# Softplus of q spread over the loop over k, a sixth of its copies on ScalarE, and row sums copied first

## The chip, the cores and the metric

The kernel runs on one core of a Trainium2 chip. The metric is the device time of one execution in microseconds; the time of the kernel before is the median of three runs. The profile is of one such execution. Its engines are TensorE (PE, with its weight loads as PEld), VectorE (DVE), ScalarE (ACT), GpSimd (POOL) and SyncE (SP), which here issues most of the DMAs.

## The reference, cut to what matters

Eight images of 256 channels and 96 x 96 pixels go through two residual layers. Layer 0 is attention between channels in the frequency domain; layer 1 is linear attention over pixels. Both begin with a group norm.

```python
# layer 0: per head of 32 channels, q, k, v are 2D FFTs of 1x1 convolutions of gn(x)
attn = einsum('bhcn,bhdn->bhcd', l2norm(q_f), l2norm(k_f)) * temperature
attn = complex(softmax(real(attn)), softmax(imag(attn)))
out  = abs(ifft2(einsum('bhcd,bhdn->bhcn', attn, v_f)))
x    = x + pconv(out, w_out)
# layer 1: q and k have 32 channels, v has 256; xf is gn(x) as (B, C, N)
q = softplus(einsum('dc,bcn->bnd', Wq, xf) + bq)
k = softplus(einsum('dc,bcn->bdn', Wk, xf) + bk)
v = einsum('ec,bcn->ben', Wv, xf) + bv
attn_map = einsum('bdn,ben->bde', k, v)
norm = 1.0 / einsum('bnd,bd->bn', q, sum(k, -1) + EPS)
x = x + einsum('bnd,bde,bn->ben', q, attn_map, norm)
```

## The kernel before

The kernel never builds the FFTs. The logits of layer 0 come from the covariance of the even and odd parts of the image, which `pair_sums` gathers (e and o are the sum and the difference of an image and its point reflection). `rotate` turns each row pair of the image by a table `tm`, which gives an image y whose channel mixing yields the absolute value of the inverse FFT; with it comes one more column per row, the row sums `ys`. `images` mixes and projects them; `layer1` and `output` are the second layer.

Each stage is a generator, and `weave` runs steps of another stage between its parts: `yield n` lets n steps of the other stage in. So the sums of image b + 1 run between the parts of `layer1(b)` and `output(b)`, and the rotation of image b between the parts of `attention(b)`. The last image has no sums beside it. A scheduler orders the instructions of each engine from this, outside the stretches that set the order by hand.

At the start, VectorE makes the constant tables before the first sums:

```python
nc.vector.reduce_sum(rep4[:, 0:D], ident.rearrange("p (j d) -> p d j", d=D), axis=AX.X)
# ... (copies to rep4, sel8)
nc.vector.memset(xT, 1.0)
# ...
for j in range(4):                       # 12 copies, of a table that a DMA brings
    o = HEAD * j
    nc.vector.tensor_copy(gsel[:, 0:16, j], gri[:, o:o + 16])
    # ...
pcs = ps_tile("pcs")                     # two small matmuls, and the rotation table from them
for c in range(2):
    nc.tensor.matmul(pcs[0:H, c:c + 1], lhsT=csn[0:1, c, :], rhs=ones[0:1, 0:1], start=True, stop=True)
```

The sums: each block u of rows gets e and o (L308, and L309 for the first column), four transposes (L341), a copy by ScalarE (L344), and the products `acc` (L322) of the block before.

```python
eng = nc.vector if u in (0, 1, NT) or b == 0 and u % 2 else nc.gpsimd
op(d[:, :, lo:hi, 1:W], x_t[:, :, ra:ra + n, 1:W], x_t[:, :, back, W - 1:0:-1])      # L308
# ... in pair_sums, for each block and each 128 columns:
nc.tensor.transpose(pt[0:np_, ...], eo[:, c, k, i:i + np_], ident)                   # L341
nc.scalar.activation(t[0:np_, :, 0:C], pt[0:np_, :]..., AF.Copy, scale=weight)       # L344
if pending is not None:
    products(*pending, first, False)                                                 # L322
```

In `attention`, the softmax of the two halves m of the heads ends in the matmuls `at` (L485), with steps of the rotation let in ahead of each:

```python
            yield (5, 2)[m]
            pa = ps_tile(f"at_{b}_{m}")
            nc.tensor.matmul(pa[:, 0:4 * NZ], lhsT=sbd, rhs=gsel..., start=True, stop=True)
```

The end of a step of `rotate`, and the first matmuls of `images` that read `ys`:

```python
nc.vector.tensor_copy(y[:, :, :, g:g + 2], src[:, :, W - 1::-1, :])     # L550
nc.vector.tensor_copy(ys[:, :, g:g + 2], src[:, :, W, :])               # L551
# images: zs = mz^T ys (L583); then the z matmuls on y (L612)
```

Layer 1, with softplus and the loop over k (six turns s of three blocks i):

```python
yield 1.5

def softplus(c, s):                      # c = 0: k, c = 1: q; z holds max(a, 0), e holds exp(-|a|)
    nc.vector.tensor_scalar_add(u, e, 1.0)                                              # L735
    nc.vector.scalar_tensor_tensor(e, in0=u, scalar=1.0, in1=e, op0=ALU.subtract, op1=ALU.subtract)  # L736
    nc.scalar.activation(u, u, AF.Ln, bias=zero)                                        # L737
    nc.vector.tensor_sub(z, z, e)                                                       # L738
    nc.vector.tensor_add(z, z, u)                                                       # L739
# ...
softplus(0, 0)
for s in range(NS):
    if s + 1 < NS:
        softplus(0, s + 1)
    if s >= NS // 2:
        for i in (0, 1):
            softplus(1, 2 * s - NS + i)
    # transpose k of turn s (kT, L764), copied by ScalarE (L765)
    for i in range(s * CH // P, (s + 1) * CH // P):
        for jj in range(2):
            # eight transposes of x (xT, L773)
            if jj:
                nc.scalar.copy(xt[jj][:, :, 0:C], src)                                  # L776
            else:
                nc.vector.tensor_copy(xt[jj][:, :, 0:C], src)                           # L778
        if len(pend) == 2:
            for p in pend:
                add_kx(*p)               # kx += k^T x (L746)
            pend = []
        pend.append((i, xt, ...))
        yield 0.25
```

All transposes and most products pass through one pool of five PSUM tiles (`ps_tile`), so a transpose also waits until the tile of five allocations before is copied out.

Of the kernel before, what the change touches and what calls it, by code (L numbers as in the profile page):

```python
# [54 lines left out]
P = 128  # L55
KC = 2
HEAD = 32
D = 32
# [10 lines left out]
def two_layer_kernel(ctx: ExitStack, tc: tile.TileContext, x, w1t, b1, w2t, b2, w3, b3, wot, temp,  # L69
# [56 lines left out]
    def ps_tile(name):  # L126
        return psum.tile([P, 512], F32, tag="ps", name=name)
# [28 lines left out]
        nc.vector.memset(mask4[s, 12 + j:D + 4:4], 1.0)  # L156
        nc.vector.memset(esel[s, j:j + 1], 1.0 / HEAD)
    rep4 = const.tile([P, P], F32, name="rep4")
    nc.vector.reduce_sum(rep4[:, 0:D], ident.rearrange("p (j d) -> p d j", d=D), axis=AX.X)
    for j in range(1, 4):  # L160
        nc.vector.tensor_copy(rep4[:, 32 * j:32 * j + 32], rep4[:, 0:D])
    sel8 = const.tile([P, 8 * D], F32, name="sel8")
    nc.vector.tensor_copy(sel8.rearrange("p (i d) -> p i d", d=D), rep4[:, 0:8].unsqueeze(2).to_broadcast([P, 8, D]))
    NX = 6
    xT = const.tile([P, NX, 2, C + 2], F32, name="xT")
    nc.vector.memset(xT, 1.0)
    turn = [0, 0]

    def xt_slot(sums=False):
# [8 lines left out]
    nc.scalar.dma_start(out=gavg_sb, in_=gavg)  # L178
    gri = setup[:, 6 * W:6 * W + 2 * P]
    nc.scalar.dma_start(out=gri, in_=gmat)  # L180
    for j in range(4):
        o = HEAD * j
        nc.vector.tensor_copy(gsel[:, 0:16, j], gri[:, o:o + 16])
        nc.vector.tensor_copy(gsel[:, 17:32, j], gri[:, P + o + 1:P + o + 16])
        nc.vector.tensor_copy(gsel[:, 32, j:j + 1], gri[:, o + 16:o + 17])
    half = const.tile([P, 1], F32, name="half")
    nc.vector.memset(half, 1.0)
    nc.vector.memset(half[0:W], 0.5 ** 0.5)
# [42 lines left out]


    rt = dram.tile([H, 2 * W], F32, name="rt")
    pcs = ps_tile("pcs")
    for c in range(2):
        nc.tensor.matmul(pcs[0:H, c:c + 1], lhsT=csn[0:1, c, :], rhs=ones[0:1, 0:1], start=True, stop=True)
    cs = t0[:, 5 * W:5 * W + 2]
    nc.vector.tensor_copy(cs, pcs[0:H, 0:2])
    r0 = t0[:, 2 * W:3 * W]
    nc.vector.tensor_scalar_mul(t0[:, 0:W], t0[:, 0:W], cs[:, 0:1])  # L240
    nc.vector.scalar_tensor_tensor(r0, in0=t0[:, W:2 * W], scalar=cs[:, 1:2], in1=t0[:, 0:W], op0=ALU.mult, op1=ALU.add)
    for i in range(2):
        o = (3 + i) * W
        nc.vector.tensor_copy(t0[:, o:o + 1], r0[:, 0:1])
        nc.vector.tensor_copy(t0[:, o + 1:o + W], r0[:, W - 1:0:-1])
    nc.sync.dma_start(out=rt, in_=t0[:, 3 * W:5 * W])
    load_small()

    def window(h):

# [37 lines left out]
    def even_odd(b, u):  # L288

        nr = PR if u < NT else 1  # L290
        t = ring_tile(f"eo_{b}_{u}").rearrange("p (c k n) -> p c k n", c=2, k=KC)
        x_t = image(x_of(b))
        rows = [PR * u + i for i in range(nr)]
        if u in (0, NT):
            parts = [(0, 1)] + ([(1, nr)] if nr > 1 else [])
        else:
            parts = [(0, nr)]
        for lo, hi in parts:
            n = hi - lo
            ra = x_col(rows[lo]) // W  # L300
            rp = x_col((H - rows[lo]) % H) // W
            back = slice(rp, rp - n if rp >= n else None, -1)
            for c in range(2):
                eng = nc.vector if u in (0, 1, NT) or b == 0 and u % 2 else nc.gpsimd
                op = (eng.tensor_add, eng.tensor_sub)[c]
                pop = (nc.gpsimd.tensor_add, nc.gpsimd.tensor_sub)[c]
                d = t[:, c, :, 0:nr * W].rearrange("p k (h w) -> p k h w", w=W)
                op(d[:, :, lo:hi, 1:W], x_t[:, :, ra:ra + n, 1:W], x_t[:, :, back, W - 1:0:-1])  # L308
                pop(d[:, :, lo:hi, 0:1], x_t[:, :, ra:ra + n, 0:1], x_t[:, :, back, 0:1])  # L309
        return t, nr * W  # L310
# [50 lines left out]
    def attention(b):  # L361
# [105 lines left out]
        for m in range(KC):  # L467
            l = two.tile([P, HEAD], F32, tag="l", name=f"l_{b}_{m}")
            for j in range(4):
                s = slice(32 * j, 32 * j + 32)  # L470
                nc.vector.tensor_mul(l[s, :], lg[m][s, s], rk[s, m * P + 32 * j:m * P + 32 * j + 32])
            nc.vector.tensor_scalar_mul(l, l, rq[:, m:m + 1])
            nmax = two.tile([P, 1], F32, tag="nmax", name=f"nmax_{b}_{m}")
            nc.vector.reduce_max(nmax, l, axis=AX.X, negate=True)
            ssum = two.tile([P, 1], F32, tag="ssum", name=f"ssum_{b}_{m}")
            nc.scalar.activation(l, l, AF.Exp, bias=nmax, accum_out=ssum)
            nc.vector.reciprocal(ssum, ssum)
            sbd = scr[0][:, 5 * C + m * P:5 * C + (m + 1) * P]
            nc.gpsimd.memset(sbd, 0.0)
            for j in range(4):  # L480
                s = slice(32 * j, 32 * j + 32)
                nc.vector.tensor_scalar_mul(sbd[s, s], l[s, :], ssum[s, :])
            yield (5, 2)[m]
            pa = ps_tile(f"at_{b}_{m}")
            nc.tensor.matmul(pa[:, 0:4 * NZ], lhsT=sbd, rhs=gsel.rearrange("p n h -> p (n h)"), start=True, stop=True)  # L485
            nc.vector.tensor_copy(at[:, m, 0:NZ, 4 * m:4 * m + 4], pa[:, 0:4 * NZ].rearrange("p (n h) -> p n h", h=4))
            nc.vector.tensor_add(at[:, m, 16, 4 * m:4 * m + 4], esel, pa[:, 64:68])
# [33 lines left out]
    def rotate(b):  # L521

        y = image(y_of(b))
        ys = one.tile([P, KC, H + 1], F32, tag="ys", name=f"ys_{b}")

        def load_r(h):
            tm = three.tile([P, TR * (W + 1)], F32, tag="tm", name=f"tm_{b}_{h}")[0:W].rearrange("p (r w) -> p r w", r=TR)
            (nc.scalar if b else nc.sync).dma_start(out=tm[:, :, 0:W], in_=window(h))
            nc.gpsimd.tensor_copy(tm[:, :, W:W + 1], csn[0:W, 2, h:h + TR].unsqueeze(2))  # L529
            return tm  # L530

        def step(h, turned):

            if h is not None:
                pt = ps_tile(f"xr_{b}_{h}")
            if turned is not None:
                g, gt, tm = turned
                pu = ps_tile(f"y_{b}_{g}")
            for r in range(2):
                for k in range(KC):  # L540
                    if h is not None:
                        o = x_col(h + r)
                        nc.tensor.transpose(pt[0:W, r * C + k * P:r * C + (k + 1) * P], x_of(b)[:, k, o:o + W], ident)  # L543
                    if turned is not None:
                        o = (r * KC + k) * (W + 1)
                        nc.tensor.matmul(pu[:, o:o + W + 1], lhsT=gt[0:W, r, k * P:(k + 1) * P], rhs=tm[:, g % TR + r, :],  # L546
                                         start=True, stop=True)
            if turned is not None:
                src = pu[:, 0:2 * KC * (W + 1)].rearrange("p (r k w) -> p k w r", r=2, k=KC)
                nc.vector.tensor_copy(y[:, :, :, g:g + 2], src[:, :, W - 1::-1, :])  # L550
                nc.vector.tensor_copy(ys[:, :, g:g + 2], src[:, :, W, :])  # L551
            if h is not None:
                xt = xt_slot()
                nc.scalar.copy(xt[0:W, :, 0:C], pt[0:W, :].rearrange("p (r n) -> p r n", r=2))  # L554
                return xt

        tms = [load_r(g) for g in range(0, 3 * TR, TR)]
        pending = []
        for h in range(0, H, 2):
            if h % TR == 0:  # L560
                tm = tms.pop(0)
            if h % TR == 4 and 3 * TR <= h - 4 + 2 * TR < H:
                tms.append(load_r(h - 4 + 2 * TR))
            xt = step(h, pending.pop(0) if len(pending) == 2 else None)
            pending.append((h, xt, tm))
            yield
        for p in pending:
            step(None, p)
        y0[b] = ys
# [101 lines left out]
    def layer1(b):  # L671
# [53 lines left out]
            nc.tensor.matmul(pv[:, 0:C], lhsT=nmb[:, k, :], rhs=wvs[:, k, :], start=(k == 0), stop=(k == KC - 1))  # L725
        nc.vector.tensor_add(bvs, bvs, pv[:, 0:C])

        yield 1.5

        def softplus(c, s):  # L730

# [24 lines left out]
        for s in range(NS):  # L756
            if s + 1 < NS:
                softplus(0, s + 1)
            if s >= NS // 2:
                for i in (0, 1):  # L760
                    softplus(1, 2 * s - NS + i)
            pk = ps_tile(f"kT_{b}_{s}")
            for i in range(CH // P):
                nc.tensor.transpose(pk[:, i * P:(i + 1) * P], kq(0, s)[:, i * P:(i + 1) * P], ident)  # L764
# [1 line left out]
            for i in range(s * CH // P, (s + 1) * CH // P):  # L766
                xt = [slots[2 * (i % 3) + jj] for jj in range(2)]
                for jj in range(2):
# [3 lines left out]
                        for k in range(KC):  # L772
                            nc.tensor.transpose(pt[:, j * C + k * P:j * C + (k + 1) * P], x[:, k, o:o + P], ident)  # L773
                    src = pt.rearrange("p (j n) -> p j n", j=2)
                    if jj:
                        nc.scalar.copy(xt[jj][:, :, 0:C], src)  # L776
                    else:
                        nc.vector.tensor_copy(xt[jj][:, :, 0:C], src)  # L778
                if len(pend) == 2:
                    for p in pend:  # L780
                        add_kx(*p)
                    pend = []
# [102 lines left out]
    def finish(stage):  # L885
        for _ in stage:
            pass

    finish(pair_sums(0))
    turns = rotate(0)  # L890
    for b in range(B):
        with tc.manual_schedule(engines={mybir.EngineType.PE}):
# [60 lines left out]
```

## Time and profile before

| | |
|---|---|
| time, median of 3 (lowest, highest) | 2787.41 us (2787.17, 2787.41) |
| span of the profiled execution | 2783.2 us |
| mean granted TensorE clock | 0.998 |
| period of one image | 342.5 us |
| HBM read and written | 113.85 MB, 75.57 MB |

The zs matmuls of two images that follow each other start 342.5 us apart (497.0 us, 839.75 us and so on), which gives the period. By line, the largest shares of the chain that ended last are the z and the projection matmuls of `images` (20% and 18%), the products of the sums (13%) and the rotation (10% and 6%); the transposes of x in the loop over k have 4%, its products kx 2%.

A line of a timeline begins with the start and the length in us; then come engine, source line, operation, tiles written and read, shape and count. Brackets hold the idle time of that engine ahead of it and what ended that. Lines of source in the profile are those of the kernel before; in the changed kernel the same statements stand a few lines lower or higher.

### The profile page before, as it was taken

What the parts mean: (1) busy time and instruction counts of PE and PEld (TensorE: products, weight loads), DVE (VectorE), ACT (ScalarE), POOL (GpSimd) and SP (SyncE); (2) the same over time, 40 slices, a digit from 0 to 9 for tenths busy, and PEclk for the clock granted to TensorE, in tenths of its full rate; (3) what the DMA queues carried; (4) which work ended last, traced back from release to release, by engine and by line L of the source; (5) the groups of instructions that cost most, each with busy time, mean ns of one, the idle gap of its engine ahead of it and who ended that gap; (6) DMA issues with size and microseconds to landing.
All of it is one profiled execution on the core that took longest, in us unless ns stands there. A gap on an engine that the chain in (4) does not pass through costs nothing.

```text
span 2783.2 us, 47916 instructions
## 1 busy us (share of the span) xinstructions
PE 2725.0 (98%) x18460; PEld 1969.4 (71%) x18460; DVE 1986.8 (71%) x4122; ACT 1350.2 (49%) x2066; POOL 858.6 (31%) x928
## 2 busy tenths in 40 slices
PE   8999999999999999999999999999999999999987
PEld 7965679656795667956679566785668856788545
DVE  6578775877658776587675876758766687666767
ACT  3455534555345553455533555345454455544553
POOL 4033430343303434034240351403514135131321
PEclk9999999999999999999999999999999999999999
DMA  5120061201512015120151201512015210151003
GB/s 167 36 67 12 25 204 40 69 10 43 183 43 72 5 48 177 44 70 7 47 180 43 69 6 53 177 48 60 7 53 181 53 51 7 55 181 30 1 6 137
DMA packets 197810, 192.52 MB, mean 69 GB/s; under 512 B 89360, under 2 KB 197584, under 8 KB 197584
## 3 DMA queue, kind: packets, MB, share of 16 engines
q1 hardware_dynamic: 130336, 164.34, 18.6%
q10 hardware_dynamic: 67248, 25.12, 3.5%
q8 instruction: 147, 2.41, 0.4%
q14 instruction: 79, 0.65, 0.1%
HBM read 113.85 MB, written 75.57 MB: 68 GB/s over the span
## 4 chain that ended last, share of the span: by engine, by line
PE 92%; DVE 4%; ACT 2%; issue 1%; POOL 0%; DMA 0%; POOLq 0%; DVEq 0%; ACTq 0%
PE z L612 20%; PE po L624 18%; PE acc L322 13%; PE y L546 10%; PE xr L543 6%; PE eoT L341 5%; PE kq L709 5%; PE xT L773 4%; PE o L855 3%; PE kx L746 2%; DVE arena L739 1%; PE cw L420 1%; DVE arena L550 1%; PE kT L764 1%; PE mz L507 1%
## 5 line engine op out<-in xcount | busy, mean ns | idle before, releaser
L612 PE MATMUL z<-arena,mz 128*128 128x384 f32 (+2 forms) x2400 | 595.0, 476 | 0.0
L624 PE MATMUL po<-e,wo 128*128 128x384 f32 x1536 | 529.7, 486 | 0.2 <-ACT e L659 0.2
L658 POOL TENSOR_TENSOR e<-e 128x768 f32<-128x768 f32 x192 | 348.5, 1817 | 553.7 <-ACT e L657 553.7
L612 PEld LDWEIGHTS z<-arena,mz 128*128 128x128 f32 (+1 forms) x2400 | 325.7, 163 | 241.4 <-issue 42.4
L546 PE MATMUL y<-tm,xT 96*128 96x97 f32 x3072 | 477.0, 261 | 1.8 <-ACT sd_a L280 0.5
L546 PEld LDWEIGHTS y<-tm,xT 96*128 96x128 f32 x3072 | 462.6, 192 | 12.4 <-ACT xT L554 5.2
L322 PE MATMUL acc<-xT 128*128 128x256 f32 (+2 forms) x2368 | 440.6, 328 | 0.0
L624 PEld LDWEIGHTS po<-e,wo 128*128 128x128 f32 x1536 | 289.5, 190 | 197.7 <-DVE arena L626 1.2
L653 DVE TENSOR_TENSOR e<-z,xT 128x768 f32<-128x768 f32 x384 | 366.1, 953 | 88.4 <-PE z L612 88.4
L256 DVE BATCH_NORM_STATS2 st<-arena 128x6 f32<-128x384 f32 x768 | 406.1, 552 | 12.6 <-DMA arena<-in_x_dram 2.2
L543 PE MATMUL xr<-ident,arena 128*96 128x128 f32 x1536 | 413.6, 275 | 0.0
L322 PEld LDWEIGHTS acc<-xT 128*128 128x128 f32 (+1 forms) x2368 | 380.1, 191 | 35.7 <-issue 2.9
L550 DVE COPY arena<-y 128x384 f32<-128x384 f32 x384 | 213.9, 557 | 209.2 <-PE y L546 203.1
L554 ACT COPY xT<-xr 96x512 f32<-96x512 f32 x384 | 222.2, 583 | 283.3 <-PE xr L543 278.9
L308 POOL TENSOR_TENSOR eo<-arena 128x760 f32<-128x760 f32 x150 | 273.4, 1823 | 258.2 <-issue 133.6
L657 ACT ACTIVATE e<-e 128x1536 f32<-128x1536 f32 x192 | 284.5, 1482 | 93.2 <-DVE e L653 92.1
L659 ACT ACTIVATE e<-e 128x768 f32<-128x768 f32 x192 | 162.0, 844 | 334.2 <-POOL e L658 333.2
L626 DVE TENSOR_TENSOR arena<-arena,po 128x384 f32<-128x384 f32 x384 | 211.3, 552 | 94.7 <-PE po L624 71.8
L344 ACT ACTIVATE xT<-eoT 128x512 f32<-128x512 f32 x280 | 167.5, 598 | 180.6 <-PE eoT L341 178.9
L529 POOL COPY tm<-csn 96x6 f32<-96x6 f32 x128 | 24.2, 192 | 726.7 <-PE y L546 548.7
L543 PEld LDWEIGHTS xr<-ident,arena 128*96 128x96 f32 x1536 | 230.1, 150 | 8.9 <-issue 5.6
L341 PE MATMUL eoT<-ident,eo 128*128 128x128 f32 (+1 forms) x1184 | 186.8, 280 | 8.2 <-DVE eo L308 5.3
(201 smaller groups left out, 2932.2 us busy)
## 6 DMA issues: line engine op xcount, KB each, us to landing
arena<-in_x_dram SPq DMA_DIRECT2D x184, 384.0 KB
out_dram<-arena SPq DMA_DIRECT2D x184, 384.0 KB
tm<-rt ACTq DMA_DIRECT2D x112, 216.0 KB
tm<-rt SPq DMA_DIRECT2D x16, 216.0 KB
arena<-in_x_dram SPq DMA_DIRECT2D x8, 288.0 KB
out_dram<-arena SPq DMA_DIRECT2D x8, 288.0 KB
wl<-in_w1t_dram SPq DMA_DIRECT2D x8, 256.0 KB
wl<-in_w2t_dram SPq DMA_DIRECT2D x8, 256.0 KB
```

What stands on the lines that cost most here:

```text
L256: nc.vector.bn_stats(out=st[:, k, c, :], in_=x_of(b)[:, k, c * CH:(c + 1) * CH])
L308: op(d[:, :, lo:hi, 1:W], x_t[:, :, ra:ra + n, 1:W], x_t[:, :, back, W - 1:0:-1])
L322: mm = nc.tensor.matmul(acc[c][:, m * C:m * C + (KC - m) * P], lhsT=t[0:np_, c, m * P:(m + 1) * P], rhs=t[0:np_, c, m * P:C], start=(first ...
L341: nc.tensor.transpose(pt[0:np_, c * C + k * P:c * C + (k + 1) * P], eo[:, c, k, i:i + np_], ident)
L543: nc.tensor.transpose(pt[0:W, r * C + k * P:r * C + (k + 1) * P], x_of(b)[:, k, o:o + W], ident)
L546: nc.tensor.matmul(pu[:, o:o + W + 1], lhsT=gt[0:W, r, k * P:(k + 1) * P], rhs=tm[:, g % TR + r, :], start=True, stop=True)
L550: nc.vector.tensor_copy(y[:, :, :, g:g + 2], src[:, :, W - 1::-1, :])
L612: mm = nc.tensor.matmul(out[:, o:o + n * W], lhsT=columns(mz, k, c, j), rhs=y[:, k, h * W:(h + n) * W], start=(k == 0 and o == 0), stop=(k ...
L624: nc.tensor.matmul(po[:, 0:CH], lhsT=wo[:, k, m * P:(m + 1) * P], rhs=e[:, k, :], start=(k == 0), stop=(k == KC - 1))
L653: nc.vector.tensor_add(e[:, 2 * c:2 * c + 2, :].rearrange("p t (q h) -> p t q h", h=H), pz[:, 0:CH].rearrange("p (q h) -> p q h", h=H).uns ...
L657: nc.scalar.activation(e, e, AF.Square)
L658: nc.gpsimd.tensor_add(e[:, 0:2, :], e[:, 0:2, :], e[:, 2:4, :])
```

## The change

It does six things. They are meant to take waits out of TensorE's way.

1. The constant tables (rep4, sel8, gsel, the rotation table and its two matmuls) are made after the first step of image 0's sums is issued; the fill of xT is cut to the two columns that need ones.
2. In the sums, for all images but the first, block u = 5 (NT // 2 - 1) has its e and o made by VectorE and not by GpSimd; this block's sums fall into the loop over k of the image before.
3. Three steps of the rotation, not two, are let in ahead of the second `at` matmul.
4. In the rotation, the row sums are copied ahead of y.
5. Two steps of sums, not 1.5, are let in between the projections of q and k and the loop over k.
6. In the loop over k, softplus of q is no longer issued two at a time ahead of each of the last three turns but one behind the second and one behind the third block of the turn; and every third block has its first copy made by ScalarE too (6 of 36 copies).

```diff
-    nc.vector.memset(xT, 1.0)
+    nc.vector.memset(xT[:, :, :, C:C + 2], 1.0)
 (rep4, sel8, gsel, pcs and the rotation table: moved as they are into tables())
+    def tables():
+        ...
-                eng = nc.vector if u in (0, 1, NT) or b == 0 and u % 2 else nc.gpsimd
+                eng = nc.vector if u in (0, 1, NT) or (u == NT // 2 - 1 if b else u % 2) else nc.gpsimd
-            yield (5, 2)[m]
+            yield (5, 3)[m]
+                nc.vector.tensor_copy(ys[:, :, g:g + 2], src[:, :, W, :])
                 nc.vector.tensor_copy(y[:, :, :, g:g + 2], src[:, :, W - 1::-1, :])
-                nc.vector.tensor_copy(ys[:, :, g:g + 2], src[:, :, W, :])
-        yield 1.5
+        yield 2
-            if s >= NS // 2:
-                for i in (0, 1):
-                    softplus(1, 2 * s - NS + i)
-                    if jj:
+                    if jj or i % 3 == 2:
                         nc.scalar.copy(xt[jj][:, :, 0:C], src)
                     else:
                         nc.vector.tensor_copy(xt[jj][:, :, 0:C], src)
+                if s >= NS // 2 and i % (CH // P):
+                    softplus(1, 2 * s - NS + i % (CH // P) - 1)
-    finish(pair_sums(0))
+    sums = pair_sums(0)
+    next(sums)
+    tables()
+    finish(sums)
```

More of the change, by code (lines that the diff above doesn't have):

```diff
@@ L158, in two_layer_kernel @@
     rep4 = const.tile([P, P], F32, name="rep4")
-    nc.vector.reduce_sum(rep4[:, 0:D], ident.rearrange("p (j d) -> p d j", d=D), axis=AX.X)
-    for j in range(1, 4):
-        nc.vector.tensor_copy(rep4[:, 32 * j:32 * j + 32], rep4[:, 0:D])
     sel8 = const.tile([P, 8 * D], F32, name="sel8")
-    nc.vector.tensor_copy(sel8.rearrange("p (i d) -> p i d", d=D), rep4[:, 0:8].unsqueeze(2).to_broadcast([P, 8, D]))
     NX = 6
     xT = const.tile([P, NX, 2, C + 2], F32, name="xT")
-    nc.vector.memset(xT, 1.0)
+    nc.vector.memset(xT[:, :, :, C:C + 2], 1.0)
     turn = [0, 0]
@@ L180, in two_layer_kernel @@
     nc.scalar.dma_start(out=gri, in_=gmat)
[L181 to L185, printed above, removed]
     half = const.tile([P, 1], F32, name="half")
@@ L233, in two_layer_kernel @@
     rt = dram.tile([H, 2 * W], F32, name="rt")
[L234 to L247, printed above, removed]
+    def tables():
+        nc.vector.reduce_sum(rep4[:, 0:D], ident.rearrange("p (j d) -> p d j", d=D), axis=AX.X)
+        for j in range(1, 4):
+            nc.vector.tensor_copy(rep4[:, 32 * j:32 * j + 32], rep4[:, 0:D])
+        nc.vector.tensor_copy(sel8.rearrange("p (i d) -> p i d", d=D), rep4[:, 0:8].unsqueeze(2).to_broadcast([P, 8, D]))
+        for j in range(4):
+            o = HEAD * j
+            nc.vector.tensor_copy(gsel[:, 0:16, j], gri[:, o:o + 16])
+            nc.vector.tensor_copy(gsel[:, 17:32, j], gri[:, P + o + 1:P + o + 16])
+            nc.vector.tensor_copy(gsel[:, 32, j:j + 1], gri[:, o + 16:o + 17])
+        pcs = ps_tile("pcs")
+        for c in range(2):
+            nc.tensor.matmul(pcs[0:H, c:c + 1], lhsT=csn[0:1, c, :], rhs=ones[0:1, 0:1], start=True, stop=True)
+        cs = t0[:, 5 * W:5 * W + 2]
+        nc.vector.tensor_copy(cs, pcs[0:H, 0:2])
+        r0 = t0[:, 2 * W:3 * W]
+        nc.vector.tensor_scalar_mul(t0[:, 0:W], t0[:, 0:W], cs[:, 0:1])
+        nc.vector.scalar_tensor_tensor(r0, in0=t0[:, W:2 * W], scalar=cs[:, 1:2], in1=t0[:, 0:W], op0=ALU.mult, op1=ALU.add)
+        for i in range(2):
+            o = (3 + i) * W
+            nc.vector.tensor_copy(t0[:, o:o + 1], r0[:, 0:1])
+            nc.vector.tensor_copy(t0[:, o + 1:o + W], r0[:, W - 1:0:-1])
+        nc.sync.dma_start(out=rt, in_=t0[:, 3 * W:5 * W])
+        load_small()
     def window(h):
```

## The prediction

> **What bounds the kernel now.** I read the busy shares first, then the chain of waits, then the waits of TensorE alone, then the timeline around each of those waits.
>
> ```profile
> PE 2725.0 (98%) x18460; PEld 1969.4 (71%) x18460; DVE 1986.8 (71%) x4122; ACT 1350.2 (49%) x2066; POOL 858.6 (31%) x928
> ...
> PE 92%; DVE 4%; ACT 2%; issue 1%; POOL 0%; DMA 0%; POOLq 0%; DVEq 0%; ACTq 0%
> ```
>
> TensorE is busy in 98% of the span, and 92% of the chain that ended last is its own work. The change touches no matmul: it moves copies, sums and reads. So all it can win is TensorE's idle time, 2783.2 - 2725.0 = 58 us, of which 12 us lie behind the last matmul (it ends at 2771 us). The waits of TensorE, over the whole run, name where the rest lies (columns: total us, times, longest):
>
> ```profile
> PE kT L764 <- DVE arena L739: 8.3, 8, 3.6
> PE zs L583 <- DVE ys L551: 6.5, 8, 0.8
> PE eoT L341 <- DVE eo L308: 5.3, 1, 5.3
> PE xT L773 <- DVE xT L778: 5.2, 7, 0.8
> ...
> PE eoT L341 <- POOL eo L309: 2.9, 8, 1.6
> PE kx L746 <- DVE xt L778: 2.7, 7, 0.4
> ...
> PE kx L746 <- DVE xT L778: 0.7, 2, 0.5
> ...
> PE at L485 <- DVE ssum L477: 0.5, 1, 0.5
> ```
>
> Four of them are what the change aims at: the row sums (zs), the first transposed k (kT), the two waits late in the loop over k (xT and kx), and the start (eoT). Together 8.3 + 6.5 + 5.3 + 5.2 + 2.7 = 28 us, 1.0% of the span. That is the ceiling, so a change of over 2% is not to be had on this side. A gap in this view is some 0.16 us smaller than the time lost against the usual pace from one matmul's start to the next, as the pipeline's end is counted as busy; below I count the pace.
>
> Image 1's loop over k, 666 to 706 us, on VectorE and GpSimd:
>
> ```profile
> 682.23 0.68 DVE L778 COPY xT<-xT 128x512 f32<-128x512 f32 x1
> ...
> 682.70 1.81 POOL L308 TENSOR_TENSOR eo<-arena 128x760 f32<-128x760 f32 x1 [16.52 <-DMA arena<-in_x_dram]
> 682.83 2.09 DVE L738 TENSOR_TENSOR arena<-arena 128x384 f32<-128x384 f32 x1
> ...
> 685.44 1.73 DVE L739 TENSOR_TENSOR arena<-arena,spu 128x384 f32<-128x384 f32 x1
> ```
>
> The same L738 and L739 take 0.54 us each elsewhere in this loop. Here each waits for GpSimd's even/odd sum (L308) to end: 1.55 + 1.19 = 2.7 us of VectorE are lost. VectorE has no idle stretch from 666.0 to 694.5, and TensorE pays at the end of that backlog:
>
> ```profile
> 691.79 1.24 PE L773 MATMUL xT<-ident,arena 128*128 128x128 f32 x8 [0.75 <-DVE xT L778]
> ...
> 693.99 0.64 PE L746 MATMUL kx<-xt,arena 128*32 128x257 f32 x8 [0.39 <-DVE xt L778]
> ```
>
> [...] the trace shows 1283 ns mean for the load ahead of the logarithm [...].
>
> **The change part by part.**
>
> *Row sums first.* At the end of the rotation the last copy of y runs 838.97 to 839.53, its ys copy (0.15 us) follows at 839.45, and zs starts at 839.75. With ys first, it starts at 838.97 in place of 839.45, so zs starts 0.48 us earlier. y itself is first read by the z matmuls at 841.14, so the later y copy holds nobody. 8 images x 0.48 = 3.8 us won.
>
> *Copies to ScalarE.* 6 of 18 first-half copies of the loop leave VectorE: 6 x 0.60 (back to back, 0.68 alone) = 3.6 us per image. ScalarE takes 6 x 0.5 = 3 us more; it was busy 23 of the 43 us of 664 to 707, so it has room, but in its order the copies now stand beside logarithms that wait for VectorE.
>
> *e and o of block 5 to VectorE.* GpSimd's two L308 of that time (1.8 us each) go; VectorE takes 2 x 0.93 = 1.9 us and is spared the 2.7 us of blocking: -0.8 us. In VectorE's order they stand near the end of the softplus of q, one on each side of its last addition.
>
> *Softplus of q spread.* No work less. In place of two softplus ahead of each of the last three turns, one comes behind the second and one behind the third block of copies. VectorE's order is then: all steps up to the copy of block 9 (11 last adds and 10 products and 10 subtractions at 0.47, 10 additions of 1 at 0.27, 6 copies at 0.60, one e at 0.9, and the copy itself 0.6) = 14.5 + 2.7 + 3.6 + 1.5 = 22.3 us from 666.0, so 688.3. TensorE, starting kT at 668.3 (next part), needs that copy at about 687.9. A wait of about 0.45 us is left there, and about 0.2 us early, where xT of block 2 needs the slot that the copy of block 0 frees at 670.9. Before, these waits cost 0.92 + 0.55 = 1.47 us against the pace. Won: 1.47 - 0.65 = 0.8 us, x 7 images = 5.7 us.
>
> *One more step of sums ahead of the loop (2 for 1.5).* It puts 1.75 us of TensorE work into the wait for kT (0.85 us against the pace). But that step's products need ScalarE's copy of the step before, and this stands behind the table load and two logarithms:
>
> ```profile
> 664.05 1.28 ACT L737 ACT_TABLE_LOAD   x1
> 665.34 1.12 ACT L737 ACTIVATE spu<-spu,own 128x384 f32<-128x384 f32 x2
> 666.37 0.58 ACT L344 ACTIVATE xT<-eoT 128x512 f32<-128x512 f32 x1
> ```
>
> The copy ends at 666.95; TensorE has done the step's transposes by 666.33 and waits some 0.70 us for it. The order of the changed kernel on ScalarE has the copy still behind both logarithms. So the wait for VectorE becomes one for ScalarE: 0.15 us x 7 = 1 us won, not 6. The loop starts 1.55 us later for TensorE, which is the head start for VectorE that the part above has used.
>
> *The start.* VectorE's 12 table copies (0.9 us) wait for a DMA until 7.35 us and stand ahead of the first even sum at 8.57. In the changed order 11 of the 12 still stand ahead of it; only the small fills (0.3 us) and one copy are gone, so it starts at about 8.2. [...] So 0.4 us earlier; the two small table matmuls, done in idle time before, now stand between the transposes. Some 0.3 us won of 5.3.
>
> *The step of attention (3 for 2).* In seven images the at matmul loses 0.3 to 0.65 us, but it is the first of the pair that waits; the change moves the second. I count 0.3 us in all.
>
> *Last image.* No sums fill its waits. The 3.6 us for kT stay (table load, logarithm, add). The late wait of 0.47 us (0.64 against the pace) goes: 0.5 us.
>
> Sum: 3.8 + 5.7 + 1.0 + 0.3 + 0.3 + 0.5 = 11.6 us. 2787.4 - 11.6 = 2775.8, so **2776 us**, 0.4% faster.
>
> **The rivals.** (a) The waits go wholly: the step fills the wait for kT and VectorE has no backlog. That adds 0.7 x 7 + 0.65 x 7 = 9.5 us: 2766. For it: VectorE loses 3.6 + 0.8 = 4.4 us of 28 in the loop. Against it: the order on ScalarE. (b) ScalarE becomes the new wait. [...] now copies stand behind logarithms that wait for VectorE, and VectorE's adds behind logarithms. One wait of 1 us per image would eat 8 us: 2784. For it: the 18 + 6 copies, 12 logarithms and 6 kT copies are 0.5 x 42 = 21 us of 28 in the last image, where no sums stretch the loop. Against it: in the middle images the loop lasts 40 us. (c) The two sums on VectorE stand ahead of the copy of block 9 and wait for their DMA or hold it longer than I think; each 0.5 us is 3.5 us in all: 2779. The rows landed at 682.7 in the profile and the sum comes up near 687, so a wait for the DMA is not likely. (d) The start loses: the table matmuls and the copies among the first statistics delay the first products by 1 us: 2777.
>
> **Range and chances.** The ceiling is 28 us (2759) and nothing adds work on TensorE. Between rival (a) and rival (b) with a little beyond: 2767 to 2785 in 8 of 10. Faster by over 2% would need 56 us, the whole idle time: 0.01. Slower by over 2% would need a new stall of 7 us in every image: 0.01. Within 2%: 0.98.
>
> **What the profile would show.** Row sums: the wait of zs falls from 0.81 to about 0.33 us, eight times. The step: kT's seven waits of 0.68 vanish and acc waits for ScalarE's xT copy 0.5 to 0.7 us in their place. Spreading: in the loop no 2 us L738, and xT and kx wait 0.65 us an image in place of 1.5. Start: first products at about 13.2 us, before 13.48. I am wrong if kT or acc do not wait at all (rival a), if copies of xT wait on ScalarE inside the loop (rival b), or if TensorE's busy time itself changes by more than a few us.

## The result, and the profile after

| | before | after |
|---|---|---|
| median of 6 runs each, us | 2787.29 (2785.42 to 2789.98) | 2777.85 (2775.90 to 2778.79) |
| span of the profiled execution, us | 2783.2 | 2776.2 |
| from one image's first row-sum matmul to the next's, mean of 7, us | 342.45 | 341.26 |

The ratio is 0.9966, with a 95% interval of 0.9953 to 0.9978: 9.4 us won where 11.4 us (2787.4 to 2776) were predicted. The total fits. Two of its terms don't, and they nearly cancel; that is what the experiments found.

The page of the changed kernel: busy time by engine, and the engines of the chain that ended last.

```profile
PE 2731.4 (98%) x18460; PEld 1982.1 (71%) x18460; DVE 1950.3 (70%) x4088; ACT 1374.4 (50%) x2114; POOL 835.8 (30%) x914
...
PE 94%; DVE 3%; ACT 2%; issue 0%; DMA 0%; POOL 0%; POOLq 0%; ACTq 0%; DVEq 0%
```

TensorE's count of matmuls is the same, and its own share of the chain went from 92% to 94%: idle time went, no work. Its busy time rose by 6.4 us (2725.0 to 2731.4) all the same, which the prediction had as a sign of being wrong: from the last image's zs on it is 207.7 us before and 216.3 after, as the clock was lower there (0.57 and 0.58 in two stretches and 0.50 in the output, where before has 0.79 in one stretch and 1.00 in its output; see the last image, below), and over the seven images ahead 1.6 us less. The waits of TensorE in the changed kernel (columns as before: total us, times, longest):

```profile
PE eoT L344 <- DVE eo L311: 9.4, 2, 9.2
PE rec L833 <- DVE rec L819: 5.2, 8, 1.6
PE kT L764 <- DVE arena L742: 3.6, 1, 3.6
PE acc L325 <- ACT xT L347: 3.5, 7, 0.5
...
PE zs L586 <- DVE ys L553: 2.0, 8, 0.3
PE kx L749 <- DVE xT L778: 2.0, 7, 0.3
PE den L816 <- DVE own L807: 1.9, 8, 0.8
PE eoT L344 <- POOL eo L312: 1.3, 7, 0.2
```

The row sums' wait fell from 6.5 to 2.0 us. kT waits once (the last image) in place of eight times, xT not at all. But three rows are new or larger: acc for ScalarE (in seven images), rec (once an image; 1.6 us in one image before) and den (0.7 us in one image before). And kx still waits for VectorE, 2.0 us in place of 2.7 + 0.7. The 9.2 us of eoT is the first wait of the run, from time 0; before, the two small table matmuls cut it in two (3.6 and 5.3 us).

The timeline of image 1 shows the new waits where they stand: at the entry of the loop over k, late in it, and behind it.

```profile
660.47 1.28 ACT L740 ACT_TABLE_LOAD   x1
...
661.76 1.12 ACT L740 ACTIVATE spu<-spu,own 128x384 f32<-128x384 f32 x2
...
662.79 1.06 ACT L347 ACTIVATE xT<-eoT 128x512 f32<-128x512 f32 x2
...
663.42 1.58 PE L325 MATMUL acc<-xT 128*128 128x256 f32 x8 [0.51 <-ACT xT L347]
...
683.39 0.94 DVE L311 TENSOR_TENSOR eo<-arena 128x760 f32<-128x760 f32 x1
...
685.08 0.64 PE L749 MATMUL kx<-xT,arena 128*32 128x257 f32 x8 [0.28 <-DVE xT L778]
...
705.93 2.56 DVE L819 RECIPROCAL rec<-den 128x384 f32<-128x384 f32 x1 [1.70 <-PE den L816]
...
707.21 0.82 PE L325 MATMUL acc<-xT 128*128 128x256 f32 x4
...
708.55 0.93 PE L833 MATMUL rec<-rec,sel 32*128 32x384 f32 x8 [0.52 <-DVE rec L819]
```

The last three lines are one story: VectorE's reciprocal takes 2.56 us, TensorE has only 4 products of the sums (0.82 us) to do under it, and rec waits. Before, 8 products lay there. The step that was let in earlier is missing here.

I measure stages from the first matmul of one line to the first of the next, in image 1 (us; the last column is the mean of seven images). xr are the transposes at the head of the rotation, kq the projections of k and q, kxT the products that turn kx behind the loop, den and rec the denominator and its reciprocal spread over the rows, o the products of the output. The labels stand with the experiments below.

| kernel | xr to zs | kq to kT | loop: kT to kxT | kxT to o | image |
|---|---|---|---|---|---|
| before | 75.23 | 23.84 | 40.23 | 9.05 | 342.45 |
| after | 74.90 | 25.51 | 37.91 | 8.76 | 341.26 |
| e_step | 74.90 | 23.85 | 37.56 | 9.05 | 339.51 |
| e_min | 74.81 | 23.84 | 38.16 | 9.04 | 339.93 |
| e_copy | 74.97 | 25.51 | 37.38 | 8.76 | 340.75 |
| e_eo | 74.90 | 25.51 | 40.86 | 8.76 | 344.06 |

The other two stages, zs to kq (145.9 to 146.0) and o to the next xr (48.1 to 48.6), don't move. Image 1 of after holds 8 matmuls of acc more than before between kq and kT (34 for 26), 4 less in the loop (40 for 44) and 4 less between den and rec (4 for 8). So the loop's 37.91 us hold half a step less than e_step's 37.56.

### The profile page after: what moved, and what is told of

Its sections match the earlier page's. It is cut to its first block, busy times and chain, and to the rows that moved or that the text cites. A ratio compares the mean times of both kernels' runs of the same rounds, so it can differ in the third digit from the quotient of the medians.

```text
span 2776.2 us, 47920 instructions
## 1 busy us (share of the span) xinstructions
PE 2731.4 (98%) x18460; PEld 1982.1 (71%) x18460; DVE 1950.3 (70%) x4088; ACT 1374.4 (50%) x2114; POOL 835.8 (30%) x914
## 4 chain that ended last, share of the span: by engine, by line
PE 94%; DVE 3%; ACT 2%; issue 0%; DMA 0%; POOL 0%; POOLq 0%; ACTq 0%; DVEq 0%
PE z L615 20%; PE po L627 18%; PE acc L325 13%; PE y L549 10%; PE xr L546 6%; PE eoT L344 5%; PE xT L773 5%; PE kq L712 5%; PE o L857 4%; PE kx L749 3%; PE cw L423 1%; DVE rec L819 1%; PE kT L764 1%; DVE arena L554 1%; PE mz L510 1%; PE cw L434 1%
## 5 line engine op out<-in xcount | busy, mean ns | idle before, releaser
L311 POOL TENSOR_TENSOR eo<-arena 128x760 f32<-128x760 f32 x136 | 247.2, 1818 | 141.9 <-issue 133.3
L553 DVE COPY ys<-y 128x4 f32<-128x4 f32 x384 | 62.5, 163 | 207.2 <-PE y L549 205.1
```

## The experiments

Theory: the waits of the loop go because VectorE no longer waits for the end of GpSimd's sums (2.7 us in L738 and L739 of image 1 of before), has fewer copies and a head start of one step. Rivals: one part does it all, or the parts give back elsewhere what they win. Each kernel below is the changed kernel with one edit, unless it says otherwise. The medians of before, run beside them on the same chips, lay at 2787.1 to 2788.8 us.

**The step undone (e_step).**

```diff
-        yield 2
+        yield 1.5
```

> The changed kernel with 1.5 in place of 2 steps of sums let in ahead of the loop over k. Theory (the half step only trades waits): the wait of acc for ScalarE's copy (0.67 us an image against the pace) goes and kT waits 0.85 us for VectorE again; the new waits of den and rec (0.32 and 0.68 us) go, as the phase of the steps is the old one; the late wait in the loop (kx, 0.45) grows by about 0.2. From the first kq to the first o: 72.2 us an image in the changed kernel, 71.6 here, so about 4 us less in all, 2774. Rival (the half step is VectorE's head start): the late waits grow by the 1.5 us that TensorE enters the loop earlier; 72.7 us an image, 2781.

Measured: 2765.59 us (2764.04 to 2767.09), ratio to before 0.9916 (0.9901 to 0.9931). Both expectations fall: it is 12.3 us faster than the changed kernel. TensorE's waits in this profile:

```profile
PE eoT L344 <- DVE eo L311: 9.3, 2, 9.1
PE kT L764 <- DVE arena L742: 8.3, 8, 3.6
...
PE zs L586 <- DVE ys L553: 2.1, 8, 0.3
PE rec L833 <- DVE rec L819: 1.6, 1, 1.6
```

The old wait of kT is back, 0.68 us seven times, and in exchange the rows of acc and kx are gone, and rec is left with the last image alone. Against the pace, an image of the changed kernel lost 0.67 us at acc, 0.87 in kx's row of matmuls, 0.59 at rec and 0.22 at den, and won 0.84 at kT: 1.5 us net of the 1.72 that the stages show, the rest in small gaps. The image as a whole is 1.75 us shorter (341.26 to 339.51), x 7 = 12.2 us, which is the whole difference. So the extra step is a loss, not a gain of 1 us.

It also shows what the other parts do in the loop with the steps of before: 40.23 to 37.56 us, 2.67 us an image, where I had counted 0.8.

**e and o of block 5 back on GpSimd (e_eo).**

```diff
-  eng = nc.vector if u in (0, 1, NT) or (u == NT // 2 - 1 if b else u % 2) else nc.gpsimd
+  eng = nc.vector if u in (0, 1, NT) or b == 0 and u % 2 else nc.gpsimd
```

> The changed kernel with e and o of block 5 on GpSimd again. Theory [...]: two of VectorE's sums in the loop take 1.7 to 2.1 us in place of 0.54, together 2.7 us, and VectorE is spared 0.9 us ahead of the copy that TensorE waits for; kx waits 0.8 to 1.8 us longer in each of seven images: kT to kxT 37.9 us becomes 38.7 to 39.7, the whole 6 to 12 us longer, 2784 to 2790. Rival (VectorE has room now): no more than 0.2 us an image, 2779.

Measured: 2797.33 us (2794.25 to 2799.13), ratio 1.0034 (1.0021 to 1.0046), 19.5 us slower than the changed kernel, and more than expected. The loop of image 1 in its timeline:

```profile
680.76 1.80 POOL L311 TENSOR_TENSOR eo<-arena 128x760 f32<-128x760 f32 x1 [14.82 <-DMA arena<-in_x_dram]
680.91 2.06 DVE L741 TENSOR_TENSOR arena<-arena 128x384 f32<-128x384 f32 x1
...
683.01 2.12 POOL L311 TENSOR_TENSOR eo<-arena 128x760 f32<-128x760 f32 x1
...
683.38 2.16 DVE L742 TENSOR_TENSOR arena<-arena,spu 128x384 f32<-128x384 f32 x1
...
686.20 0.64 PE L749 MATMUL kx<-xT,arena 128*32 128x257 f32 x8 [1.29 <-DVE xT L778]
...
689.05 1.15 PE L773 MATMUL xT<-ident,arena 128*128 128x128 f32 x8 [0.86 <-ACT xt L776]
...
691.37 0.64 PE L749 MATMUL kx<-xT,arena 128*32 128x257 f32 x8 [0.60 <-ACT xT L776]
```

L741 and L742 take 2.06 and 2.16 us in place of 0.54: each ends 0.41 us behind GpSimd's sum (682.97 and 682.56 us, 685.54 and 685.13). VectorE is late, the loop's kx waits 1.29 us, and now ScalarE's copies come late too (0.86, 0.60), as they stand behind logarithms that waited 2.25 and 2.77 us for VectorE. 2.8 us an image x 7 = 19.6 us. This one part carries the change: without it the rest is 9.5 us slower than the kernel before on this chip (2787.86).

**The six copies back on VectorE (e_copy).**

```diff
-  if jj or i % 3 == 2:
+  if jj:
```

> The changed kernel with the six copies of the loop back on VectorE. Theory (VectorE's backlog sets the late wait): three of the six stand ahead of the copy of block 9, 1.8 us; the waits of xT and kx grow by about that, kT to kxT 37.9 becomes 39.7, the whole 12 us longer, 2790. Rival (ScalarE's in-order copies cost as much as they free): kT to kxT within 0.5 us of 37.9, and the last image's loop, where ScalarE is fullest, is shorter by 1 us.

Measured: 2772.81 us (2772.46 to 2773.09), ratio 0.9942 (0.9927 to 0.9957): 5.0 us faster, where the theory had it slower; the rival, a loop within 0.5 us of 37.9, comes near. The row of kx is gone from the waits, and the loop takes 37.38 in place of 37.91 us. With the copies on ScalarE, VectorE's sum e (683.39 above) stands ahead of both copies of the pair of blocks, and kx waits for them; with them on VectorE the copies stand between the additions. 0.5 us x 7 = 3.5. The rest lies in the last image of the profile, and not in the copies: its loop takes 30.99 us here and 30.75 in e_start, where they are on ScalarE. It goes with the clock, which is at 0.50 for 3.4 us about the start of that loop in both (see the last image, below).

**Softplus of q two at a time, as before (e_sp).**

```diff
+            if s >= NS // 2:
+                for i in (0, 1):
+                    softplus(1, 2 * s - NS + i)
             pk = ps_tile(f"kT_{b}_{s}")
...
-                if s >= NS // 2 and i % (CH // P):
-                    softplus(1, 2 * s - NS + i % (CH // P) - 1)
```

> The changed kernel with softplus of q two at a time ahead of each of the last three turns, as before; copies, sums and steps as changed. Theory (VectorE's total ahead of block 9's copy counts, and the scheduler brings all six softplus of q ahead of it in either way): kT to kxT within 0.5 us of 37.9, the whole within 3 us of 2778. Rival (the spreading takes the waits away): the old waits of xT and kx, 1.5 us an image in place of 0.45, come back: 2785.

Measured: 2776.93 us (2774.95 to 2778.06), ratio 0.9956 (0.9941 to 0.9971); an image takes 341.3 us, the loop 37.91. As expected, the same: the part that gives the change its name is worth nothing here. It was not undone alone with the step of before.

**y copied before ys (e_ys).**

```diff
-  nc.vector.tensor_copy(ys[:, :, g:g + 2], src[:, :, W, :])
   nc.vector.tensor_copy(y[:, :, :, g:g + 2], src[:, :, W - 1::-1, :])
+  nc.vector.tensor_copy(ys[:, :, g:g + 2], src[:, :, W, :])
```

> The changed kernel with y copied ahead of the row sums again. Theory: zs waits 1.0 us against the pace in place of 0.45 in each of eight images; from the first xr to zs 74.9 becomes 75.45, the whole 4.4 us longer, 2782. Rival (the order costs something elsewhere in the rotation, as the step from xr to zs fell by only 0.35): 75.25 us and 2.8 us.

Measured: 2780.92 us (2779.93 to 2782.71), ratio 0.9972 (0.9961 to 0.9984): 3.1 us slower than the changed kernel. The stage from xr to zs takes 75.33 for 74.90 us, between theory and rival, and in the first image 76.25 for 75.16: 0.43 x 7 + 1.1 = 4.1. The part does what it was made for.

**The attention's third step undone (e_at).**

```diff
-  yield (5, 3)[m]
+  yield (5, 2)[m]
```

> The changed kernel with 2 steps of the rotation ahead of the second at matmul, as before. Theory (the third step gains nothing, the first at is the one that waits): from xr to zs 74.9 us stays within 0.2 us, the first at waits 0.34 us as before, the whole within 2 us of 2778. Rival (it takes a wait of the second at away that the ys order would bring): 0.3 us an image longer, 2780.

Measured: 2778.25 us (2775.61 to 2778.45), ratio 0.9958 (0.9942 to 0.9975). In the time no difference; in the stage from xr to zs 74.72 us for 74.90, so the third step costs 0.18 us an image rather than winning. 1.3 us in seven images is less than the runs scatter.

**The tables ahead of the first sums (e_start).**

```diff
+    tables()
     sums = pair_sums(0)
-    next(sums)
-    tables()
     finish(sums)
```

> The changed kernel with the tables made ahead of the first sums, as before. Theory [...]: VectorE's first sum begins at 8.3 to 8.5 us[...]; the first xr is at 78.2 to 78.4 us in place of 77.0, the whole 1.3 us longer. Rival (it is the two small matmuls or the fill): the first xr within 0.5 us of 77.0.

Measured: 2775.52 us (2774.08 to 2775.57), ratio 0.995 (0.9935 to 0.9965): 2.3 us faster, not slower. The first xr is at 76.80 us for 76.97, so the rival has the time. The start of before and of the changed kernel, from their timelines:

```profile
8.15 0.14 DVE L185 COPY gsel<-arena 128x1 f32<-128x1 f32 x1
8.24 0.06 DVE L187 MEMSET half<- 128x1 f32 x1
...
8.38 0.16 DVE L192 MEMSET hw<- 1x1 f32 x2
8.57 3.41 DVE L308 TENSOR_TENSOR eo<-arena 128x760 f32<-128x760 f32 x2
8.89 2.29 POOL L308 TENSOR_TENSOR eo<-arena 128x760 f32<-128x760 f32 x1 [2.49 <-DMA arena<-in_x_dram]
```

```profile
8.08 1.80 DVE L311 TENSOR_TENSOR eo<-arena 128x760 f32<-128x760 f32 x2
8.88 2.65 POOL L311 TENSOR_TENSOR eo<-arena 128x760 f32<-128x760 f32 x1 [2.48 <-DMA arena<-in_x_dram]
...
10.61 0.80 PE L239 MATMUL pcs<-ones,csn 1*96 1x1 f32 x4
11.34 1.33 PE L344 MATMUL eoT<-ident,eo 128*128 128x128 f32 x5
...
12.46 1.91 PE L325 MATMUL acc<-xT 128*128 128x256 f32 x5
```

VectorE's two sums take 1.80 us together, and it is GpSimd's that takes 2.65 in place of 1.8. Before, VectorE's pair took 3.41 us, its second sum behind GpSimd's. But the table matmuls (0.80) now stand between the transposes. With the tables ahead, VectorE's sums began at 8.21 and took 1.80 all the same, no table matmul stood there, and the first products came at 11.68 in place of 12.46.

So it was not the moved tables that turned the start and, by the timelines, not the fill of xT: before, that ran from 2.37 to 5.01 us, while VectorE had to wait until 7.35 for the DMA of the tables. In the timelines one other thing differs. Before, small fills of constants (0.3 us, the lines of MEMSET above) stand between the table copies and the first sum. In the changed kernel, and in this one, `tables()` is called behind them, and they are done by 2.7 us. That they alone turn the start was not run. Moving the tables behind the first sums costs something in its turn: the two kernels with the tables first (this one and e_min) have their first xr at 76.80 and 76.35 us, the eleven with the tables moved at 76.97 to 78.72, 77.9 in the mean.

Of the 2.8 us between the two profiled spans, only 0.2 are won by the first xr; 2.6 lie in the last image, below.

**More steps earlier (e_early).** One step ahead of the last read of the exponentials, one ahead of the loop.

```diff
+        yield 1
         zero = own[:, 5 * C:5 * C + 1]
...
-        yield 2
+        yield 1
```

> The changed kernel with one of the two steps of sums let in ahead of the scalar that the logarithm takes as its bias, and one behind the bvs matmuls. ScalarE's order then has the copy that acc needs between the first and the second logarithm, and no longer behind both. Theory: the copy is done 0.5 us earlier, acc waits 0.15 in place of 0.67 us against the pace in seven images: 3.6 us less, 2774. Rival (the wait moves to kT, as the second logarithm comes later): the same within 1 us.

Measured: 2775.78 us (2775.28 to 2776.40), ratio 0.9957 (0.9944 to 0.9971). An image takes 341.2 us as in the changed kernel. Its waits show why:

```profile
PE rec L834 <- DVE rec L820: 5.2, 8, 1.6
PE xT L774 <- ACT xT L777: 4.8, 7, 0.7
```

The rival is right that an image takes the same time, but named kT. acc no longer waits for ScalarE, but TensorE is then early at the transposes of the first blocks, and those wait 0.7 us an image for ScalarE's copies, which in image 1 stand behind a logarithm that itself waited 1.01 us for VectorE. The wait has moved from the entry into the loop: 0.49 us less from kq to kT, 0.47 more in the loop.

**One step more under the reciprocal (e_fill).** At the end of `layer1`:

```diff
-        yield 1
+        yield 2
         l1[b] = x, kq, rec, am
```

> The changed kernel with two steps of sums in place of one let in at the end of layer 1, between den and rec. Theory (the new wait of rec, 0.68 us against the pace, is for want of a step there): rec waits no more and den still 0.32; from den to the first o one step (1.75 us) more less 0.68, and one step less after the output: 7 x 0.68 = 4.8 us less, 2773. Rival (the step is then missing later and another wait takes its place): the same within 1.5 us.

Measured: 2772.44 us (2772.33 to 2774.91), ratio 0.9948 (0.9933 to 0.9964), as expected. An image takes 340.61 us, 0.65 less: rec's wait is gone in the seven images. It pays back a part of what the extra step took.

**A busy TensorE in the last image (e_warm).** Matmuls whose results nobody reads, 7 behind the last projection and 14 behind bvs, in the last image only, to keep the clock up through the waits there (cut to the matmuls).

```diff
+  for n in range(7):
+      nc.tensor.matmul(pw[:, 0:CH], lhsT=wo[:, 0, 0:P], rhs=p[1][:, 0, :], start=True, stop=True)
...
+  for n in range(14):
+      nc.tensor.matmul(pw[:, 0:C], lhsT=nmb[:, 0, :], rhs=wvs[:, 0, :], start=True, stop=True)
```

> The changed kernel with 7 idle matmuls behind the last projection of the last image and 14 behind its bvs matmuls, in the two waits of that image; their results are not read. Theory (the last image lost 3 to 4 us to TensorE's halved clock after these waits): the halved stretches in its kq and loop go, kq to kT 24.1 becomes 22.8 and kT to kxT 31.9 becomes 29.1, the whole 4 us shorter, 2774. Rival (ScalarE's copies lengthen that loop): both stay within 0.3 us, the whole the same or longer.

Measured: 2780.09 us (2778.90 to 2782.71), ratio 0.997 (0.9958 to 0.9981): 2.2 us over the changed kernel's median, no gain. The busy time in stretches of the last image (stretch, length, busy us and instructions of PE, PEld, DVE, ACT, POOL; then the granted clock, the DMA share and GB/s). The changed kernel:

```profile
2680.00:2688.00 8.00, 7.37 (x78) 3.24 (x82) 2.50 (x8) 2.25 (x4) 0.00 (x0) 0.57 0.02 3
2704.00:2712.00 8.00, 7.16 (x45) 6.24 (x46) 5.59 (x12) 4.56 (x9) 0.00 (x0) 0.58 0.00 0
```

And with the added matmuls:

```profile
2680.00:2688.00 8.00, 6.80 (x87) 3.81 (x89) 3.06 (x13) 1.34 (x4) 0.00 (x0) 1.00 0.01 3
2704.00:2712.00 8.00, 6.92 (x49) 6.02 (x51) 7.38 (x17) 4.56 (x9) 0.00 (x0) 1.00 0.00 0
```

The clock does stay at 1.00 there, for 0.57 and 0.58 in the changed kernel: with TensorE's waits filled, the half clock is gone. But the matmuls themselves take about as long as they save: from zs to kq 141.31 us for 139.80, then 0.7 won up to kT and 1.3 in the loop. That nets 0.5 us against this profile of the changed kernel; from zs to kxT it is 195.3 us, and kernels without the added matmuls took 192.4 to 195.8 (the last image, below), so in most cases they cost more than they save.

**All three of these together (e_best):** early, fill and the added matmuls.

> The three together: a step ahead of the logarithms, two steps at the end of layer 1, and the idle matmuls in the last image. If they add up: 3.6 + 4.8 + 4 = 12.4 us less than the changed kernel, 2765.5. If ScalarE's copy or the missing step costs it back, 2770 or more.

Measured: 2775.48 us (2774.05 to 2776.41), ratio 0.9956 (0.9944 to 0.9969). They don't add: an image takes 340.57 us, as with the fill alone, and the whole is 3 us slower than with the fill alone: the added matmuls are in it.

**Three parts alone (e_min).** The kernel before with the row sums first, e and o of block 5 on VectorE, and the small fill of xT; everything else, the tables ahead of the first sums too, as before, but for `tables()`, which stands behind the small fills of constants here too.

> The kernel before with three parts of the change only: the row sums copied first, e and o of block 5 on VectorE, the small fill at the start. No copies to ScalarE, softplus of q two at a time, the old steps (1.5 ahead of the loop over k, 5 and 2 in the attention), the tables ahead of the first sums. From the profiles: with the step undone an image takes 339.43 us against 341.2, with the attention's step undone 0.18 less; over eight images and with some 0.8 us of the start that is 2765.6 - 1.4 - 0.8 = 2763.4. Theory: GpSimd's two sums were all that held the loop over k, and the other parts add nothing there; then kx and xT do not wait in the loop, it takes 37.6 us an image as with the step undone, and the whole 2763. Rival A: the copies on ScalarE cost 0.54 us an image here too, then 37.0 us and 2759.5. Rival B: with 3.6 us of copies more on VectorE and no head start the backlog is back, xT or kx waits 0.5 us or more an image, the loop takes 38.2 us or more and the whole 2767 or more.

Measured: 2768.84 us (2767.96 to 2769.94), ratio 0.9934 (0.992 to 0.9948), 9 us faster than the whole change. The theory is nearly right and not quite: the loop takes 38.16 us, 2.07 less than before, but 0.6 more than e_step's. Rival B had the loop's time, but not the wait it named. The loss lies early in the loop, in one row of kx:

```profile
667.50 0.57 ACT L779 COPY xt<-xT 128x512 f32<-128x512 f32 x1
...
669.09 0.67 DVE L781 COPY xT<-xT 128x512 f32<-128x512 f32 x1
669.25 0.61 ACT L740 ACTIVATE spu<-spu,own 128x384 f32<-128x384 f32 x1 [0.80 <-DVE arena L739]
...
669.77 1.05 ACT L779 COPY xT<-xT 128x512 f32<-128x512 f32 x2
669.87 0.17 PEld L749 LDWEIGHTS kx<-xT,arena 128*32 128x32 f32 x4 [0.39 <-ACT spu L740]
```

ScalarE's copy stands behind a logarithm that waited 0.80 us for VectorE, and VectorE was late by copies that e_step has on ScalarE. So the six copies are worth 0.6 us an image with the old step (with softplus of q spread in the same kernel, which alone did nothing) and cost 0.5 with the new one.

## Why the prediction was right, and which of its terms were not

The mechanism that should win was named, the ceiling held, and the time fell into the range. That it fell near 2776 is luck, as two of the terms show. By the prediction's own terms, in us won over the whole run:

| term | predicted | measured, and from where |
|---|---|---|
| row sums first | 3.8 | xr to zs 75.25 to 74.72 us with the old attention step: 0.53 x 8 = 4.2, and 0.6 more in the first image |
| loop: spreading, copies, e and o | 5.7 | before to e_step: 2.6 x 7 = 18 |
| one more step ahead of the loop | 1.0 | e_step to after: -1.75 x 7 = -12.2 |
| start | 0.3 | first products 13.48 to 12.46; first xr 78.4 to 77.0: 1.4 (0.4 against 78.0, the mean of the ten other kernels with this start) |
| third attention step | 0.3 | -0.18 x 7 = -1.3 by the stage; not visible in the time |
| last image | 0.5 | zs to kxT 192.4 to 195.8, output 0.3: -3.8 |

These sum to 6.9 us; the two profiled spans differ by 7.0. The medians differ by 9.4: the profiled span lies 4.1 us under the median before, and 1.7 after. The profiled execution of before is one of its quicker ones: of the 38 runs of before made beside the experiments, the 13 with a mean clock of 0.997 or 0.998, as in the profile, took 2786.3 us in the median, the 25 with 0.992 or 0.993 took 2788.8.

*The loop was mis-sized* by more than a factor of three. The step "before, these waits cost 0.92 + 0.55 = 1.47 us" counted only the two waits that the list names. Matmul by matmul, against the pace of e_step, image 1 of before lost 1.40 us in the row of kx (I had 0.55), 0.92 at xT, and 0.33 between transposes. The wait of "about 0.45 us" that I left at the copy of block 9 came (the longest gap in kx is 0.44 against the pace), but it comes with the new step: with the old one no wait is left there. So the term should have been 1.40 + 0.92 + 0.33 = 2.65 us an image with nothing left over, where I had 1.47 - 0.65.

*The step of sums failed in sign.* Its arithmetic at the entry held: TensorE "waits some 0.70 us for it" came out as 0.67, in exchange for 0.84 at kT. What I left out is that a step let in ahead of the loop is missing later. The loop has half a step less, so TensorE catches VectorE up at kx, and the other half is missing under the 2.56 us reciprocal, where rec and den now wait. I counted the later start of the loop as "the head start for VectorE", and did not ask what would fill the stages behind it.

Loop and step together win 0.88 us an image (2.63 - 1.75), 6.2 us, where the prediction had 6.7: the sum was right by luck, because two errors of 12 and 13 us cancelled.

*Rivals.* (b), ScalarE as the new wait, came true at the entry alone, 0.67 us an image at acc, as the prediction's own term had it; inside the loop of the changed kernel TensorE waits for VectorE. (c) came true at kx, 0.87 us an image: the sum e stands ahead of the copies there. (a) is e_step's state, apart from kT's wait: 2766 was its figure, 2765.6 was measured, by other terms than it had added. (d) came true in part: the table matmuls put the first products at 12.46 us where they come at 11.68 with the tables first; the start as a whole still won.

*The start.* I had left the second sum of VectorE's pair behind GpSimd's first one, as it was before; in all thirteen other profiles it came ahead. In both starts the later of the two sums ended as if it had begun when the other was done: before, VectorE's second sum ended 0.80 us after GpSimd's (11.98 and 11.18 us), and after, GpSimd's first ended 1.65 us after VectorE's pair (11.53 and 9.88), each close to what one such sum takes alone (0.9 and 1.8). VectorE's second sum came last where its first led GpSimd's by 0.32 us, and first with leads of 0.55 to 0.86; why the lead should decide, no run here shows.

*The last image* was to win 0.5 us and lost 3.8 in these two profiles. That is the clock and not the loop. The clock column has a stretch at half there:

```profile
2690.00:2698.00 8.00, 6.91 (x88) 3.33 (x92) 2.98 (x10) 2.17 (x4) 0.00 (x0) 0.79 0.01 2
```

A mean of 0.79 over 8 us is some 3.4 us at half clock (0.50; 8 x 0.21 / 0.5); that is all that before has ahead of its output. The changed kernel has two stretches, 0.57 and 0.58 above, some 6.8 us each. In slices of 0.5 us, each such stretch of the twelve kernels without the added matmuls lasts 3.4 or 6.8 us, and nothing between. Eight of these kernels do the same from the last zs on, and the time that they take goes with the stretches:

| kernels | at half clock from zs to kxT, us | zs to kxT, us |
|---|---|---|
| e_eo | 6.8 | 192.4 |
| e_ys, e_start | 3.4 + 3.4 | 193.0, 193.3 |
| e_early, e_fill | 6.8 + 3.4 | 193.8, 193.8 |
| e_at, e_step, after | 6.8 + 6.8 | 195.6, 195.8, 195.8 |

e_eo's last image is as long as that of before (192.4), and its loop, with no stretch at half clock in it as in before, takes 29.08 us for 29.86: there the term was right, 0.8 us for 0.5. Ahead of the first stretch of the changed kernel TensorE waited 2.73 us, and then 0.93; ahead of the second, 3.60. What sets when the clock is halved, and which of the two lengths (6.8 is twice 3.4) an execution gets, is not shown.

## What to carry to other kernels

Filler work let in ahead of one wait is taken from under another: before moving it, list the waits behind the place it leaves, down to the longest instruction it used to cover. When several parts are changed at once, a sum that comes out right proves none of its terms; undo each part alone, as here one part (e and o away from GpSimd) carried the change, one was worth nothing, and one cost more than half of the gain. The version to keep, of those measured, is the change without the extra step: 2765.6 us, 0.8% under before. The third attention step undone and the tables first, each of which looked better here, were not run together with it.

## What the runs showed of the hardware that was not expected

- Sums of VectorE and GpSimd side by side at the start went either way: VectorE's pair of sums took 3.41 us with a start at 8.57, and 1.80 us with starts from 7.94 to 8.43; GpSimd's sum beside it took 2.29 us, and then 2.6 to 2.9 us.
- Gaps too small to be listed as waits added up: in the loop of before, 0.85 us an image in kx alone, beside the 0.55 us that could be seen at once.
- In the last image TensorE's clock was halved, ahead of the output, for 3.4 or for 6.8 us at a time and for nothing between, in twelve profiles. In the changed kernel it came behind waits of 2.73 and 0.93 us, and again behind one of 3.60 us (kT); behind that last wait no such stretch came in two of the twelve (before and e_eo).
- Kernels with the same start differ by up to 1.7 us at the first xr (77.0 to 78.7 us), and with the same last image by 3.5 us. A difference of 2 us between two of these kernels says little by itself; the stages of the seven middle images mostly repeat within 0.1 us, with single images 0.3 to 0.5 us off, and say much.
